# Reordering the dense steps of the second block: projections, transposes, scores, mixed values, feed-forward

## The chip, the cores and the metric

One core of a Trainium2 chip. The metric is the device time of one execution in microseconds (us). Five engines work side by side, each through its own queue in order: TensorE (PE) multiplies matrices, VectorE (DVE), ScalarE (ACT) and GpSimd (POOL) work element by element, SyncE (SP) issues DMAs. They wait for each other through semaphores.

## The reference

Two blocks work on x (2 batches of 1024 tokens, 256 features). The first block (attention over all tokens, then a mixture of 64 experts) isn't touched here. The second is `x = x + L1_ffn(L1_cond(x))`; L1_cond is a rotation of x, and L1_ffn has two layers of this form (cut):

```python
def _layer(x, wqkv, qs, ksc, wo, lg, lb, w1, b1, w2, b2):
    h = shift_token(x)                     # half of the features one token late
    q, k, v = split(h @ wqkv)              # 8 heads of 64
    q, k = l2norm(q) * qs, l2norm(k) * ksc
    q, k = rotary_xpos(q, k)               # cos/sin tables, times a scale by position
    o = local_attention(q, k, v)           # each token: itself and the 128 before
    x = x + o @ wo
    h = layernorm(shift_token(x)) * lg + lb
    a, g = split(h @ w1 + b1)
    return x + (a * gelu(g)) @ w2 + b2
```

Everything is float32.

## The kernel before

The second block runs over 32 windows of 128 tokens (2 layers x 2 batches x 8) and over 8 chunks of 512 tokens for the feed-forward. One loop, `for s in range(-2, WINDOWS)`, is a software pipeline: step s projects window s + 2, turns (transposes) queries and keys of window s + 1, scores window s, turns the softmax weights e of window s - 1, mixes values for window s - 2 or s - 1, and does a quarter of the feed-forward of a chunk that lags seven steps (LAG = 7). The order of the Python calls is the order on PE, DVE, ACT and POOL: `tc.manual_schedule` names these engines, so nothing is moved by a scheduler. Steps up to s = 4 also carry the rest of the first block (`beside`); from s = 5 to 29 a step is called dense; the last two are `late`.

The pieces, with the names that the profile uses (lines of the kernel before):

- `project(i)` L1146: pq, 4 matmuls of 128x128 by 512 (float32 goes twice through the array, so 8 records). `rotate_parts(i)`: ACT copies pq to raw (L1176) and squares it (sq, L1177), DVE multiplies pq by the cosines (L1164), POOL raw by the sines (t2, two operations, L1184). `norms(i)`: DVE sums the squares (L1193 and two small ones), POOL takes three Newton steps of four small operations (L1200 to L1203) to zn, the reciprocal norms. `rotated(i)`: DVE adds cosines and sines (L1209) and multiplies the keys by zn (L1210).
- `values(i)` L1216: pv, 2 matmuls; `keep_values(i)`: ACT copies it (L1226).
- `turn(i)`: 16 transposes of 64 rows into pt (L1231), two ACT copies to qT and kT (L1242); every third window POOL copies kT (L1247).
- `scores(i, hg)` L1259: sc for half the heads, matmuls of 64x64 by 192. `maxima(i, hg)`: DVE adds the mask, scales and takes the maximum (L1280, four each). `weights(i, hg)`: ACT takes exp (L1297, four each). `divide(i, hg)`: a DVE reciprocal (L1309), then four products (L1313), on POOL for hg 0 and on DVE for hg 1.
- `turn_e(i, hg)`: 16 transposes into pe (8 where the window is the first of its batch; L1231), copied to eT by ACT for hg 0 (L1334) and by DVE for hg 1 (L1332).
- `mix(i, hg)` L1347: po, 8 matmuls on 64 columns each; after hg 1 ACT copies to oT (L1358).
- `project_out(g)` L1367: pwo, 8 matmuls of 512, once in four windows, added on DVE (L1371); `halves(f)`: POOL adds the two feature halves (L1383).
- `forward(at)`: quarter k of chunk f. k = 0: gates 0, 1; k = 1: gates 2, 3; k = 2: gate 4, `centre` of the next chunk, gate 5; k = 3: `normalise`, `normalised` of the next chunk, `feed`. A `gate` is pga (L1436; the last, narrow one L1444), gelu on ACT (L1448), a product u on DVE (L1449). `centre` is pm (L1390), two subtractions on DVE (L1398), a square on ACT (L1400), a sum on POOL (L1402). `normalise` is pvar (L1390) and two ACT operations (L1410, L1411); `normalised` a product on DVE (L1417) and two operations on POOL (L1419). `feed` is py (L1463, L1468).
- `weights2(l, ...)`: DMAs of a layer's weights and tables on SP (L1044, L1052). For "tabs" it also issues four products on POOL (L1046) that scale the two tables by q_scale and k_scale. For the second layer it is called with "tabs" and "wqkv" in step 13, behind `norms` and ahead of `project_out` and `halves`.

PSUM banks in this block: `two_banks` hands out three pairs in turn, to pq, sc, pe, pt, pwo, pga and py in the order in which they are asked for, so each waits for the readers of the third one before it. `bank` hands out two single banks in turn, to pv, po, pm and pvar. eT has three buffers.

The order of PE's work in a dense step before: pq, sc (both halves), [mix of s - 2, what is left], pe of hg 0, pv, pt, [pwo], pe of hg 1, the quarter of the feed-forward.

Of the kernel before, what the change touches and what calls it, by code (L numbers as in the profile page):

```python
# [93 lines left out]
def tile_kernel(ctx: ExitStack, tc: tile.TileContext, a: dict, out: bass.AP):  # L94
# [899 lines left out]
    with tc.manual_schedule(  # L994
        engines={mybir.EngineType.PE, mybir.EngineType.DVE, mybir.EngineType.Activation}
    ):
        at_weigh = (1, 3, 4, 6)
        for g in range(2):
            weights(g)
        for it in range(3, ITS):  # L1000
            n, m = divmod(it, 8)
            if it + 1 < ITS:
                logits(it + 1)
            dispatch(it)
            if n and m in (1, 4):
                experts(4 * n - 4 + m // 4 * 2)

            i = it - ITS + 8
            if 0 <= i < 4:
                for jj in range(4):  # L1010
                    fetch(i, jj)
            if i - 1 in at_weigh:
                scale(at_weigh.index(i - 1))
            if i in at_weigh:
                heaviest(at_weigh.index(i))
                weigh(at_weigh.index(i))
        turn_w(0, 0)
        experts(12)
        turn_w(0, 1)
        combine(0, 0)  # L1020
        turn_w(0, 2)
        combine(0, 1)
        turn_w(0, 3)
        combine(0, 2)
        experts(14)
        dxs.close()
        for t in (xa, xb):
            nc.gpsimd.memset(t[:, :, :, 0:1], 0.0)


        load = {}
        wqo = pphi.tile([P, 4 * D * 4], F32, tag="phi", name="wqo")
        load["wqkv"] = wqo[:, : 6 * INNER].rearrange("p (k n) -> p k n", k=2)
        load["wo"] = wqo[:, 6 * INNER :].rearrange("p (k n) -> p k n", k=4)
        mask = dx0.tile([P, 2 * KEYS], F32, tag="l1", name="mask")
        nc.sync.dma_start(mask, a["mask"])

        def weights2(l, *names):
            for name in names:
                if name == "tabs":  # L1040

                    load[name] = [dx0.tile([P, 2, 8, DH], F32, tag="dsp", name=f"tabs{l}{y}") for y in range(2)]
                    for y, t in enumerate(load[name]):
                        nc.sync.dma_start(t, a["tabs"].rearrange("p (x y) w d -> y p x w d", y=2)[y])  # L1044
                        for x, of in enumerate((("qs", "ks"), ("qsr", "ksr"))[y]):
                            nc.gpsimd.tensor_tensor(  # L1046
                                t[:, x], t[:, x], bcast(rows[:, ROWS[f"{of}{l}"]], 1, 8), ALU.mult
                            )
                    continue
                k = {"wqkv": 2, "wo": 4, "w1": 2, "w2": NF}[name]  # L1050
                whole = HID // P if name == "w2" else k
                nc.sync.dma_start(  # L1052
                    load[name][:, :whole, :], a[name][l, : whole * P].rearrange("(c p) n -> p c n", p=P)
                )
                if whole < k:
                    for r0 in (0, TG):
                        nc.sync.dma_start(load[name][r0 : r0 + TAIL, whole, :], a[name][l, whole * P :])

        weights2(0, "wqkv", "tabs", "wo")
    with tc.manual_schedule(  # L1060
        engines={mybir.EngineType.PE, mybir.EngineType.DVE, mybir.EngineType.Activation}
    ):
# [35 lines left out]
    with tc.manual_schedule(  # L1098
# [125 lines left out]
        def keep_values(i):  # L1224
            vs[i] = la.tile([P, INNER], F32, tag="v", name="v", bufs=6)
            nc.scalar.copy(vs[i], pvs.pop(i))  # L1226
# [154 lines left out]
        def halves(f):  # L1381
            l, b, t0 = chunk(f)
            nc.gpsimd.tensor_tensor(  # L1383
                fa["sq"][:, 0, :], shifted(xb, 0, b, t0, 512), shifted(xb, 1, b, t0, 512), ALU.add
            )
# [138 lines left out]
                nc.vector.scalar_tensor_tensor(yo, py, col(f"b2{l}", c), yo, ALU.add, ALU.add)  # L1524
                nc.sync.dma_start(out[c * P : (c + 1) * P, b * S + t0 + lo : b * S + t0 + lo + m], yo)

        def forward(at):

            f, k = divmod(at, 4)
            if at == -1:  # L1530
                normalise(0)
            if not 0 <= f < CHUNKS:
                return
            if k == 0:
                gate(f, 0)
                gate(f, 1)
            if k == 1:
                gate(f, 2)
                gate(f, 3)
            if k == 2:  # L1540
                gate(f, 4)
                if f + 1 < CHUNKS:
                    centre(f + 1)
                gate(f, 5)
            if k == 3:
                if f + 1 < CHUNKS:
                    normalise(f + 1)
                    normalised(f + 1)
                feed(f)


# [28 lines left out]

        LAG = 7
        fa = {}
        for s in range(-2, WINDOWS):
            now, before, nxt, new = (0 <= s + d < WINDOWS for d in (0, -1, 1, 2))

            if new:
                project(s + 2)
                rotate_parts(s + 2)

            if s == LAG - 1:  # L1590
                centre(0)
            if s == LAG:
                normalised(0)
            ended = 0 <= s - 2 < WINDOWS

            late = s >= WINDOWS - 2
            dense = s > max(PARTS) and not late
            if ended and not dense and not late:  # L1600
                mix(s - 2, 1)
            if now and dense:
                for hg in range(2):
                    scores(s, hg)
            if ended and dense:
                for hg in range(2):
                    if (s - 2, hg) in eTs:
                        mix(s - 2, hg)
            if s == 5:
                rotate(3)  # L1610
            if now and not dense and not late:
                scores(s, 0)
                maxima(s, 0)
            beside(s, "a")
            if before:
                turn_e(s - 1, 0)
            if now and not late:
                if dense:
                    maxima(s, 0)
                weights(s, 0)  # L1620
            if new:
                values(s + 2)
                keep_values(s + 2)
            beside(s, "c")
            if ended and late:
                for hg in range(2):
                    if (s - 2, hg) in eTs:
                        mix(s - 2, hg)
            if now:
                for hg in () if dense else (0, 1) if late else (1,):  # L1630
                    scores(s, hg)
                for hg in (0, 1) if late else (1,):
                    maxima(s, hg)
                    if hg == 0:
                        weights(s, 0)
            if before and not dense:
                mix(s - 1, 0)
            if nxt:
                turn(s + 1)
            if now:  # L1640
                weights(s, 1)
            if new:
                norms(s + 2)
            if s + 2 == B * NWIN - 1:
                weights2(1, "tabs", "wqkv")
            beside(s, "b")
            if 0 <= s - 2 < WINDOWS and (s - 2) % 4 == 3:
                project_out((s - 2) // 4)
                if (s - 2) // 4 in halved:
                    halves((s - 2) // 4)  # L1650
            if before:
                turn_e(s - 1, 1)
            if now:
                divide(s, 0)
            if new:
                rotated(s + 2)
            if s == 5:

                f = xp.tile([P, 4 * NS], F32, tag="e", name="f")
                at = 0  # L1660
                for name, k, n in (("u", NF, 512), ("w2", NF, D), ("yo", 2, 512), ("rs", 1, 512), ("sq", 2, 512), ("gl", 2, 512)):
                    fa[name] = f[:, at : at + k * n].rearrange("p (k n) -> p k n", k=k)
                    at += k * n
                fa["rs"] = fa["rs"][:, 0, :]
                fa["hc"] = xin.tile([P, 2, 2, 512], F32, tag="x1", name="hc")
                load["w2"] = fa["w2"]
                load["w1"] = xp.tile([P, NE // 4 * D], F32, tag="y1", name="w1")[:, : 2 * W1N].rearrange(
                    "p (k n) -> p k n", k=2
                )
                weights2(0, "w1", "w2")  # L1670
            forward(s - LAG)
            if now:
                divide(s, 1)
            beside(s, "e")
            if s == B * NWIN + 2:
                weights2(1, "wo")
            if s == LAG + 4 * (CHUNKS // 2) - 2:
                weights2(1, "w1")
            if s == LAG + 4 * (CHUNKS // 2) - 1:
                weights2(1, "w2")  # L1680


        w, f = WINDOWS - 1, CHUNKS - 2
# [136 lines left out]
```

## Time and profile before

| | us |
|---|---|
| median of 3 runs | 1564.66 (1563.07 to 1564.69) |
| the profiled execution, device time | 1566.07 |
| its span, first to last instruction | 1563.9 |
| TensorE's mean granted clock | 0.997 |
| dense step 7 (gates 0 and 1), from pq to the next pq | 17.55 |
| dense step 21 (pwo, gate 4, centre, gate 5) | 23.90 |
| dense step 22 (normalise, feed) | 21.28 |

A line of the timeline gives start, modelled duration, engine, line of the kernel, operation, output <- inputs, the tile form (rows x columns), shape and count, and in brackets the idle time before it with what ended it. Ends on PE are modelled and overlap the next group; the distance from start to start is the time that a group takes. A line of the waits gives who waited for whom, the total in us, how many times, and the longest. The granted clock is the share of full speed that the chip let TensorE have.

### The profile page before, as it was taken

To read this page: it belongs to the slowest core of one execution; us is meant where nothing else is said; L and a number is where in the kernel's file an instruction comes from. 1 tells how busy PE (TensorE), PEld (TensorE's weight loads), DVE (VectorE), ACT (ScalarE), POOL (GpSimd) and SP (SyncE) were. 2 spreads that over 40 slices of the span, in tenths; PEclk is the share of its full clock that TensorE was granted. 3 is DMA by queue.
4 is the path that set the end of the run, shared out by engine and by line. 5 is a ranking of instruction groups with operands and counts; after the bars stand their busy time and mean duration, and the time that the engine had idled before them with its cause. 6 is when DMAs were issued, how large, how long until landed. Compare 5 with 4: busy or idle time off the path is not lost.

```text
span 1563.9 us, 25919 instructions
## 1 busy us (share of the span) xinstructions
PE 1543.9 (99%) x10176; PEld 753.1 (48%) x10176; DVE 885.4 (57%) x1606; ACT 881.3 (56%) x1710; POOL 526.7 (34%) x863
## 2 busy tenths in 40 slices
PE   8999999999999999999999999999999999999999
PEld 4333433333333444444776566555545454545544
DVE  5868768776873222225455756656556565656532
ACT  2478768787886222225233544766646666666641
POOL 4333323333330100000102344555555555555401
PEclk9999999999999999999999999999999999999999
DMA  5100010000000544445742102000100001000001
GB/s 163 55 14 14 1 21 8 6 16 8 2 1 28 167 139 152 148 151 181 241 128 88 55 1 84 2 1 1 68 1 1 15 1 51 6 1 28 14 15 40
DMA packets 49865, 82.80 MB, mean 53 GB/s; under 512 B 4552, under 2 KB 25328, under 8 KB 49488
## 3 DMA queue, kind: packets, MB, share of 16 engines
q1 hardware_dynamic: 47200, 75.31, 15.7%
q0 software_dynamic: 1584, 5.29, 1.1%
q8 instruction: 80, 1.31, 0.3%
q10 hardware_dynamic: 960, 0.56, 0.1%
q14 instruction: 41, 0.34, 0.1%
HBM read 55.97 MB, written 20.97 MB: 49 GB/s over the span
## 4 chain that ended last, share of the span: by engine, by line
PE 96%; DVE 1%; POOL 1%; ACT 1%; DMA 1%; issue 0%; ACTq 0%; DVEq 0%; POOLq 0%
PE sc L346 9%; PE pga L1436 9%; PE po L364 8%; PE pm L312 7%; PE lg L815 7%; PE pq L1146 7%; PE cmb L934 7%; PE sl L841 7%; PE py L1463 4%; PE pv L1216 4%; PE po L1347 4%; PE pwo L1367 3%; PE sc L1259 3%; PE pe L1231 2%; PE pqk L282 2%; PE py L862 2%
## 5 line engine op out<-in xcount | busy, mean ns | idle before, releaser
L319 DVE TENSOR_REDUCE mx<-pm 128x2 f32<-128x1024 f32 x256 | 301.5, 1219 | 108.1 <-PE pm L312 108.0
L354 ACT ACTIVATE e<-sc 128x512 f32<-128x512 f32 (+1 forms) x500 | 263.6, 614 | 67.8 <-PE pm L312 63.6
L346 PE MATMUL sc<-qs,km 32*128 32x512 f32 x1024 | 247.7, 616 | 0.7 <-ACT cg L564 0.7
L312 PE MATMUL pm<-km,qm 32*128 32x512 f32 x1024 | 242.8, 616 | 0.0
L382 POOL TENSOR_TENSOR ob<-ob,part 128x512 f32<-128x512 f32 x101 | 128.5, 1272 | 251.2 <-ACT part L381 251.2
L1436 PE MATMUL pga<-hc,w 128*128 128x512 f32 x320 | 143.8, 600 | 0.0
L364 PE MATMUL po<-e,v 128*32 128x512 f32 x1024 | 136.8, 604 | 0.0
L346 PEld LDWEIGHTS sc<-qs,km 32*128 32x128 f32 x1024 | 91.5, 183 | 86.6 <-ACT e L354 65.2
L1313 POOL TENSOR_SCALAR eall<-eall,den 128x192 f32<-128x192 f32 (+1 forms) x128 | 114.3, 906 | 26.9 <-DVE den L1309 26.9
L934 PE MATMUL cmb<-xb,y 128*128 128x256 f32 x512 | 118.7, 384 | 0.6 <-ACT xb L920 0.6
L1146 PE MATMUL pq<-wqo,xa 128*128 128x512 f32 x256 | 116.8, 599 | 2.2 <-ACT xb L920 1.2
L815 PE MATMUL lg<-phi,xa 128*128 128x512 f32 x256 | 116.1, 595 | 0.0
L841 PE MATMUL sl<-dsp,xb 128*128 128x512 f32 x256 | 114.9, 592 | 0.0
L1297 ACT ACTIVATE eall<-eall,nmx 128x192 f32<-128x192 f32 (+1 forms) x256 | 111.7, 442 | 4.3 <-DVE nmx L1280 4.1
L312 PEld LDWEIGHTS pm<-km,qm 32*128 32x128 f32 x1024 | 83.2, 183 | 49.3 <-DVE mx L319 35.0
L1184 POOL TENSOR_TENSOR t<-raw,tabs 128x512 f32<-128x512 f32 x64 | 80.6, 1281 | 75.1 <-ACT raw L1176 74.9
L825 DVE TENSOR_TENSOR l<-lg,keep 128x512 f32<-128x512 f32 x32 | 22.1, 692 | 144.8 <-ACT keep L823 144.8
L934 PEld LDWEIGHTS cmb<-xb,y 128*128 128x128 f32 x512 | 94.9, 189 | 17.7 <-issue 3.2
L1176 ACT COPY raw<-pq 128x1024 f32<-128x1024 f32 x32 | 32.4, 1013 | 110.5 <-PE pq L1146 109.8
L1436 PEld LDWEIGHTS pga<-hc,w 128*128 128x128 f32 x320 | 58.9, 190 | 68.1 <-issue 63.8
L1280 DVE CUSTOM_DVE_ANT_0 eall<-sc,mask,zn 128x192 f32<-128x192 f32 (+1 forms) x256 | 87.1, 404 | 4.8 <-PE sc L1259 4.7
L823 ACT COPY keep<-lg 128x512 f32<-128x512 f32 x32 | 18.7, 584 | 126.0 <-issue 105.4
(229 smaller groups left out, 2368.7 us busy)
## 6 DMA issues: line engine op xcount, KB each, us to landing
lgd<-keep SPq DMA_DIRECT2D x64, 256.0 KB, 2.4
w<-in_ffn_W SPq DMA_DIRECT2D x16, 1024.0 KB, 7.2
ebig<-lgd SPq DMA_DIRECT2D x64, 256.0 KB, 3.3
wqo<-in_wqkv SPq DMA_DIRECT2D x2, 1536.0 KB, 8.1
w<-in_w SPq DMA_DIRECT2D x2, 1386.0 KB, 7.5
km<-hk SPq DMA_DIRECT2D x32, 64.0 KB, 2.3
qm<-hq SPq DMA_DIRECT2D x32, 64.0 KB, 2.3
phi<-in_phi SPq DMA_DIRECT2D x1, 2048.0 KB, 7.4
```

Source lines behind the costliest of these rows:

```text
L312: nc.tensor.matmul(pm[:, x, :], qm[u % 2][r, i * P : (i + 1) * P], km[u % 3][r, n * 512 : (n + 1) * 512], start=True, stop=True,)
L319: nc.vector.tensor_reduce(mxs[hu][:, i % 4, 2 * half : 2 * half + 2, n], pm, AX.X, ALU.max)
L346: nc.tensor.matmul(sc[:, x, :] if both else sc[x], km[u % 3][r, j * P : (j + 1) * P], qs[u % 2][r, n * 512 : (n + 1) * 512], start=True, s ...
L354: nc.scalar.activation(part, t, AF.Exp, scale=1.0 / HD0**0.5)
L364: nc.tensor.matmul(po[32 * hh : 32 * hh + 32, :], v[b][:, j, at : at + 32], es[s, hh // 2][:, hh % 2, :], start=True, stop=True,)
L382: nc.gpsimd.tensor_tensor(obs[u, n], obs[u, n], part, ALU.add)
L815: nc.tensor.matmul(lg[:, b, :], xa[:, k, b, 1 + m * P : 1 + (m + 1) * P], phi[:, k, n * 512 : (n + 1) * 512], start=(k == 0), stop=(k == 1),)
L841: nc.tensor.matmul(accs[n][b][:, c, :], xo_tm[:, b * 8 + m, c * P : (c + 1) * P], d[:, b, :], start=(m == 0), stop=(m == 7),)
L934: nc.tensor.matmul(acs[q][:, c, :], y[b][:, 4 * jj + j, c * P : (c + 1) * P], eT[:, j // 2, j % 2 * 256 : (j % 2 + 1) * 256], start=(jj == ...
L1146: nc.tensor.matmul(pq[:, x, :], shifted(xa, k, b, w * WIN, P), load["wqkv"][:, k, x * 512 : (x + 1) * 512], start=(k == 0), stop=(k == 1),)
L1313: engine.tensor_scalar(e[:, x, c, lo:KEYS], e[:, x, c, lo:KEYS], den[:, x, c : c + 1], None, ALU.mult)
L1436: nc.tensor.matmul(pt[:, x, :], load["w1"][:, k, lo : lo + P], hcs[f][:, k, :], start=(k == 0), stop=(k == 1))
```

## The change

A function `dense_step(s)` takes over steps 5 to 29; the other steps keep the old order, without their dense branches. Its order on PE: pq, [what is left to mix of s - 2], [pwo], pv, pe of hg 0, pe of hg 1, pt, sc of both halves, po of window s - 1, the quarter of the feed-forward. `centre(0)` and `normalised(0)` of steps 6 and 7 stay at the head of the step. `forward` gets an argument `between`, called inside the quarter, through which `rotated(s + 2)` is issued. The scaling of the tables becomes a name of its own, "scales", issued behind `divide`, while the DMAs of tables and wqkv are issued behind `keep_values`. The tiles and DMAs of the feed-forward's weights are issued within step 5 rather than at its end.

```diff
+                    continue
+                if name == "scales":
+                    for y, t in enumerate(load["tabs"]):
                         for x, of in enumerate((("qs", "ks"), ("qsr", "ksr"))[y]):
                             nc.gpsimd.tensor_tensor(
                                 t[:, x], t[:, x], bcast(rows[:, ROWS[f"{of}{l}"]], 1, 8), ALU.mult
...
-        weights2(0, "wqkv", "tabs", "wo")
+        weights2(0, "wqkv", "tabs", "scales", "wo")
...
-        def forward(at):
+        def forward(at, between=lambda: None):
...
             if not 0 <= f < CHUNKS:
+                between()
                 return
             if k == 0:
                 gate(f, 0)
+                between()
                 gate(f, 1)
             if k == 1:
                 gate(f, 2)
+                between()
                 gate(f, 3)
             if k == 2:
+                between()
                 gate(f, 4)
...
                     normalised(f + 1)
+                between()
                 feed(f)
...
+        def dense_step(s):
             if s == LAG - 1:
                 centre(0)
             if s == LAG:
                 normalised(0)
+            project(s + 2)
+            rotate_parts(s + 2)
+            for hg in range(2):
+                if (s - 2, hg) in eTs:
+                    mix(s - 2, hg)
+            if s == 5:
+                rotate(3)
+            if (s - 2) % 4 == 3:
+                project_out((s - 2) // 4)
+                if (s - 2) // 4 in halved:
+                    halves((s - 2) // 4)
+            if s == 5:
+                feed_forward_tiles()
+            values(s + 2)
+            turn_e(s - 1, 0)
+            turn_e(s - 1, 1)
+            turn(s + 1)
+            keep_values(s + 2)
+            last = s + 2 == B * NWIN - 1
+            if last:
+                weights2(1, "tabs", "wqkv")
+            for hg in range(2):
+                scores(s, hg)
+            for hg in range(2):
+                maxima(s, hg)
+                weights(s, hg)
+            for hg in range(2):
+                mix(s - 1, hg)
+            norms(s + 2)
+            for hg in range(2):
+                divide(s, hg)
+            if last:
+                weights2(1, "scales")
+            forward(s - LAG, lambda: rotated(s + 2))
...
         for s in range(-2, WINDOWS):
...
+            if dense:
+                dense_step(s)
+                continue
...
-            if now and dense:
-                for hg in range(2):
-                    scores(s, hg)
-            if ended and dense:
-                for hg in range(2):
-                    if (s - 2, hg) in eTs:
-                        mix(s - 2, hg)
...
-            if s + 2 == B * NWIN - 1:
-                weights2(1, "tabs", "wqkv")
```

## The prediction

> **What bounds the kernel now.** First the page's busy times and its chain: TensorE (PE) is busy 99% of the span and holds 96% of the chain. No other engine is near it (DVE 57%, ACT 56%, POOL 34%), so only PE's own time counts: what its groups take, what it waits, and its clock.
>
> ```profile
> PE 1543.9 (99%) x10176; PEld 753.1 (48%) x10176; DVE 885.4 (57%) x1606; ACT 881.3 (56%) x1710; POOL 526.7 (34%) x863
> PE 96%; DVE 1%; POOL 1%; ACT 1%; DMA 1%; issue 0%; ACTq 0%; DVEq 0%; POOLq 0%
> ```
>
> Then PE's timeline of one ordinary step (s = 7). Start to start each group tells its true length, because the modelled ends overlap the next group.
>
> ```profile
> 1002.57 3.60 PE L1146 MATMUL pq<-wqo,xa 128*128 128x512 f32 x8
> 1006.10 1.53 PE L1259 MATMUL sc<-kT,qT 64*64 64x192 f32 x32
> 1007.56 1.97 PE L1347 MATMUL po<-eT,v 128*64 128x128 f32 x32
> 1009.46 0.71 PE L1231 MATMUL pe<-ident,eall 64*128 64x64 f32 x16
> 1010.10 1.98 PE L1216 MATMUL pv<-wqo,xa 128*128 128x512 f32 x4
> 1012.01 0.71 PE L1231 MATMUL pt<-ident,t 64*128 64x64 f32 x16
> 1012.56 0.66 PE L1231 MATMUL pe<-ident,eall 64*128 64x64 f32 x16
> 1013.15 7.13 PE L1436 MATMUL pga<-hc,w 128*128 128x512 f32 x16
> 1020.12 3.60 PE L1146 MATMUL pq<-wqo,xa 128*128 128x512 f32 x8
> ```
>
> No idle, 17.55 us. Inside a long row one full pass takes 0.427 us (pga pieces of the stage at 1220 to 1226 us: 0.85 for 2, 1.72 for 4). pv's 4 passes take 1.91 instead of 1.71: some 0.20 is the change of form, about 0.10 on the way in and 0.10 out. Transposes are 0.50 per 16, plus 0.05 in and 0.09 out (0.55 after pv and before pe, 0.64 between full forms).
>
> Third, PE's waits. The one large wait is at step 13, where the second layer's tables come in.
>
> ```profile
> PE pm L1390 <- POOL f L1383: 3.3, 1, 3.3
> ```
> ```profile
> 1133.64 6.38 POOL L1046 TENSOR_TENSOR tabs<-tabs,rows 128x512 f32<-128x512 f32 x4
> 1134.09 3.70 PE L1436 MATMUL pga<-hc,w 128*128 128x512 f32 x8
> 1139.99 1.09 POOL L1383 TENSOR_TENSOR f<-xb 128x512 f32<-128x512 f32 x1
> 1141.13 2.08 PE L1390 MATMUL pm<-f,ones_d 128*128 128x512 f32 x2 [3.34 <-POOL f L1383]
> 1143.00 3.62 PE L1444 MATMUL pga<-hc,w 128*106 128x512 f32 x4
> 1146.41 3.94 PE L1146 MATMUL pq<-wqo,xa 128*128 128x512 f32 x8
> ```
>
> Four scalings on POOL stand ahead of halves, which pm needs. After the wait L1444 takes 3.41 us for its usual 1.72: the granted clock is 0.50 for 6.8 us. The stretch from pga to the next pq is 12.32 us against 6.11 in the same stage at 1220.11, and pq itself 3.87 against 3.53: this seam costs 6.21 + 0.34 = 6.55 us.
>
> Last, how little idleness costs the clock.
>
> ```profile
> 892.41 0.71 PE L910 MATMUL pe<-ident,ebig 64*128 64x64 f32 x16 [0.87 <-DVE t L1164]
> 893.85 0.46 PE L1231 MATMUL pe<-ident,eall 64*128 64x64 f32 x8 [0.72 <-DVE nmx L1280]
> 894.24 3.55 PE L1216 MATMUL pv<-wqo,xa 128*128 128x512 f32 x4
> ```
>
> Waits of 0.87 and 0.72 us close together: the clock is 0.50 from 894.5 to 897.9, and pv takes 3.48 instead of 1.91. A wait of 0.61 beside 1.2 us of transposes (926.8 to 928.6) costs no clock. [...]
>
> **The change, part by part.** Times in a step are counted from the start of its first scores.
>
> Tables behind halves: the scalings move behind halves and behind the division of group 0, so the 6.55 us go. Late next are the scaled tables: on POOL the divisions end at 12.3, two scalings (1.3 to 1.6 each, L1046) at 15.2, the cosines (DVE 1.22) at 16.5. Step 14's turning of the queries and keys takes pq's bank and waits for them; it would stand at 15.8. Cost 0.6, bounds 0 and 2.5 (with a fall of the clock). Behind the scalings POOL has centre's addition (needed by pvar at 20.2, ready at 20.0), the copy of u's tail and the next sines; slower scalings would cost there, within the upper bound. On SP the DMAs of tables and wqkv have nothing behind them until wo, and start after the step's sines and after pv; wqkv has 11.3 us until the next pq (8.1 to land in the page), so it stays hidden. **-5.9** (-6.5 to -4).
>
> Rows: no instruction is added to PE, only groups change neighbours. An ordinary step becomes pq 3.42, pv 1.81 (no way in), pe 0.55, pe 0.50, pt 0.55, sc 1.46, po 1.90, pga 6.95 = 17.14, 0.41 less. But sc takes over the bank of the first pe, whose copy on ACT (1.01, L1334) starts 0.75 after that pe's start (L920 on the same form: 946.93 to 947.68) and ends at 1.76, 0.06 to PE: sc starts at 1.82 where it could at 1.60. All of PE's step is queued behind that wait. The second sc waits for DVE's copy (0.55 + 0.70 + 1.22 + 0.06 = 2.53) and could start at 2.55: nothing. 0.19 is left, x16 steps = 3.0. In a step with pwo two rows are joined: 23.90 becomes 23.13, less 0.22: 0.55 x3; x3 of 0.77 where only one window is turned, and the copy is 0.59. With steps 5, 6 and 7 (0.53, 0.19, 0.19) the rows bring **-7.9**. The passage from pt to sc is in no row; I take that of transposes into po (0.59 at 1482.00) and as bounds none and the 0.12 of the way into a full form: -10 to -4, if sc's wait doesn't hide it.
>
> New waits at the seams: turning e of group 0 needs POOL's division, and the old order had 20.9 us between sc and it; now it has the gates, pq and pv between, 15.5 us. Chain (durations from the groups of DVE, ACT and POOL between 960 and 1470 us): maxima 0.9 to 3.6 (8 of 0.338), sum of squares and two small ones 1.7, Newton on POOL 3.5 (12 small operations, 978.09 to 981.59), zn at 8.8, divisions to 12 or 12.7. That is enough where gates stand between, not in three places. Step 6 (only pm and pq, pv stand between: 10.4): DVE's rotated waits for zn (9.55), centre's two subtractions behind it end at 10.85, ACT's square 1.06, and queued behind that square raw 1.01, sq 1.06, the copy of e 1.01: sc at 15.07 instead of 12.2: +2.85. Step 7: rotated, normalised 1.22, cosines, then raw, sq, the copy: sc at 15.25 instead of 12.25: +3.0. Step 30, where project and values are over (pe at 9.5): rotated, u of gate 4 (0.75), the subtractions, the square, gelu 0.69, u of gate 5: the second sc at 14.5 and po at 15.3 instead of 11.5; 0.3 idle there falls away: +3.5. Each empties PE for some 3 us within 4.5, so by the row at 893 the clock falls once for 3.4 us, 1.7 lost each. That of step 6 lies in step 7's wait and costs nothing more: +3.4 (0 to 8). Together **+12.7** (8 to 18).
>
> [...]
>
> [...]
>
> w1, w2 and the other tiles of the feed-forward are issued earlier in step 5, used in step 7; the last mix of a window moves from the step after next to the next; every one of their instructions was there before. Nothing.
>
> Sum: -5.9 - 7.9 + 12.7 = -1.1 us. The profiled execution took 1566.07 (span 1563.9 and 2.2 around it) and would take 1565.0; it lies 1.4 above the median shown, 1564.66, so the median becomes 1563.6.
>
> **The rivals.** (a) The seams cost no clock, and about half their wait (POOL divides at 0.75 instead of 0.94, subtractions come earlier): -1.1 - 3.4 - 4 = 1556. For it: the 0.61 waits cost nothing. Against: three chains of in-order queues, worked out from rows. [...] (c) The rows save nothing, as the passages cost the same wherever they stand: +7.9, 1571.5. Against: pga to pq (6.97 for 6.83) pays on one side only.
>
> **How the numbers follow.** Forecast 0.45, (a) 0.23, (b) 0.15, (c) 0.17. Likeliest: 1563.6, on its own 1558 to 1570. Within 0.2% (3.1 us, about what a measurement here can tell from no change) lie 0.30, nearly all the forecast's; faster 0.32: (a) and 0.09 of the forecast; slower 0.38: (b), (c) and 0.06. The range takes in (a) and (c) and leaves out most of (b): 1556 to 1578.
>
> **What would show it.** Tables right: PE's wait pm <- POOL gone, no clock of 0.50 in step 13. Rows right: pq, pv, pe, pe, pt, sc, po in 10.4 us from pq's start to pga's, with 0.2 of wait before sc <- ACT eT. Seams right: PE waits of about 3 us in steps 6, 7 and 30, first on POOL's division, then on ACT's copy, with the clock at 0.50 behind. Wrong: no such waits (then (a)), or a granted clock under 0.98 between 1050 and 1450 us (then (b)).

## The result, and the profile after

| | us |
|---|---|
| median before (4 runs beside it) | 1564.68 (1563.07 to 1566.69) |
| median after (4 runs) | 1576.41 (1576.06 to 1577.68) |
| ratio, 95% interval | 1.0082 (1.0070 to 1.0095) |
| span of the profiled execution, before and after | 1563.9 and 1574.2 |

The change made the kernel 0.8% slower. Three single executions far from all others (2229.5 us with e2, 3966.0 with e9, 2753.6 of the kernel before beside e15) are left out of every ratio here and below. The page of the changed kernel, its busy times and its chain by engine:

```profile
PE 1541.1 (98%) x10176; PEld 756.0 (48%) x10176; DVE 883.3 (56%) x1606; ACT 881.7 (56%) x1710; POOL 535.9 (34%) x863
PE 90%; DVE 4%; POOL 2%; ACT 2%; issue 1%; DMA 1%; ACTq 0%; POOLq 0%; DVEq 0%
```

The number of instructions on each engine is the same and PE is 2.8 us less busy, but its part of the chain fell from 96% to 90%: DVE, POOL and ACT now stand in it. PE's waits between 800 us and the end say where (who waited for whom: total, times, longest):

```profile
PE pe L1234 <- POOL eall L1316: 7.3, 11, 1.7
PE pt L1234 <- DVE t L1167: 4.5, 5, 1.3
PE pe L1234 <- DVE f L1452: 2.2, 3, 0.7
...
PE sc L1262 <- ACT eT L1337: 0.6, 1, 0.6
```

The wait of pm on POOL (3.3) is gone. The division of the exponentials (L1316) is the largest new one, the cosines (L1167) and u (L1452) are the others, and once the copy of the turned exponentials (L1337): 14.6 us of waits in place of 3.3. (All lines are later by three: L1231 of before is L1234.)

PE's timeline in steps 6 and 7 of the changed kernel:

```profile
990.68 3.60 PE L1149 MATMUL pq<-wqo,xa 128*128 128x512 f32 x8
994.11 1.88 PE L1219 MATMUL pv<-wqo,xa 128*128 128x512 f32 x4
996.84 0.28 PE L1234 MATMUL pe<-ident,eall 64*128 64x64 f32 x2 [0.85 <-POOL eall L1316]
997.58 0.27 PE L1234 MATMUL pe<-ident,eall 64*128 64x64 f32 x2 [0.47 <-POOL eall L1316]
...
1000.74 1.11 PE L1234 MATMUL pt<-ident,t 64*128 64x64 f32 x16
1001.78 2.83 PE L1262 MATMUL sc<-kT,qT 64*64 64x192 f32 x32
...
1015.22 0.27 PE L1234 MATMUL pe<-ident,eall 64*128 64x64 f32 x2 [1.09 <-POOL eall L1316]
...
1018.82 2.84 PE L1262 MATMUL sc<-kT,qT 64*64 64x192 f32 x32 [0.60 <-ACT eT L1337]
```

The first transposes come two by two, each pair behind one product of POOL (0.74 us apart): 2.16 us idle in step 6 and 2.03 in step 7, where sc waits another 0.60 for ACT's copy. Behind each of the two seams sc takes 2.8 us instead of 1.46. The windows of these two steps (length, PE's busy time and records, PEld, DVE, ACT, POOL, and then PE's granted clock) give the clock's price:

```profile
988.86:1008.47 19.61, 17.43 (x135) 10.36 (x134) 13.38 (x41) 12.14 (x34) 10.27 (x21) 0.83 0.00 1
1008.47:1030.67 22.20, 19.51 (x142) 10.76 (x141) 13.77 (x36) 13.93 (x29) 16.84 (x34) 0.92 0.01 1
```

The time lost is the part of the clock that was not granted: 0.17 x 19.61 + 0.08 x 22.20 = 5.1 us, more than the waits (4.8).

An ordinary step (s = 12):

```profile
1110.29 3.60 PE L1149 MATMUL pq<-wqo,xa 128*128 128x512 f32 x8
1113.72 1.88 PE L1219 MATMUL pv<-wqo,xa 128*128 128x512 f32 x4
1115.54 1.21 PE L1234 MATMUL pe<-ident,eall 64*128 64x64 f32 x32
1116.58 0.66 PE L1234 MATMUL pt<-ident,t 64*128 64x64 f32 x16
1117.36 1.59 PE L1262 MATMUL sc<-kT,qT 64*64 64x192 f32 x32
1118.88 1.97 PE L1350 MATMUL po<-eT,v 128*64 128x128 f32 x32
1120.78 7.13 PE L1439 MATMUL pga<-hc,w 128*128 128x512 f32 x16
1127.75 3.60 PE L1149 MATMUL pq<-wqo,xa 128*128 128x512 f32 x8
```

17.46 us, 0.09 less than before (17.55). pt to sc is 0.78 where 0.55 would do: the wait for ACT's copy of pe.

The step behind a centring (s = 10; pvar and feed) has stalls that the old order had not. First the three groups of transposes before, without a wait, then PE of the changed kernel, then its DVE in the stretch that leads to the stalls:

```profile
1066.70 0.71 PE L1231 MATMUL pe<-ident,eall 64*128 64x64 f32 x16
...
1069.26 0.71 PE L1231 MATMUL pt<-ident,t 64*128 64x64 f32 x16
1069.81 0.66 PE L1231 MATMUL pe<-ident,eall 64*128 64x64 f32 x16
```

```profile
1075.00 0.71 PE L1234 MATMUL pe<-ident,eall 64*128 64x64 f32 x16
1076.43 0.71 PE L1234 MATMUL pe<-ident,eall 64*128 64x64 f32 x16 [0.72 <-DVE f L1452]
1077.95 0.71 PE L1234 MATMUL pt<-ident,t 64*128 64x64 f32 x16 [0.81 <-DVE t L1167]
1078.68 1.53 PE L1262 MATMUL sc<-kT,qT 64*64 64x192 f32 x32
```
```profile
1068.98 1.21 DVE L1212 TENSOR_TENSOR t<-t,t 128x1024 f32<-128x1024 f32 x1
1071.19 0.69 DVE L1213 TENSOR_TENSOR t<-t,zn 128x512 f32<-128x512 f32 x1 [1.00 <-POOL zn L1206]
1071.80 0.75 DVE L1452 SCALAR_TENSOR_TENSOR f<-pga,cols,f 128x512 f32<-128x512 f32 x1
1072.46 1.28 DVE L1401 TENSOR_TENSOR hc<-xb,pm 128x512 f32<-128x512 f32 x2
1075.63 0.74 DVE L1452 SCALAR_TENSOR_TENSOR f<-pga,cols,f 42x512 f32<-42x512 f32 x1 [1.89 <-ACT f L1451]
1076.67 1.23 DVE L1167 TENSOR_TENSOR t<-pq,tabs 128x1024 f32<-128x1024 f32 x1 [0.29 <-ACT raw L1179]
```

Read downwards it is one chain: the rotation waits for zn; u of gate 4 and the centring's subtractions stand behind it on DVE, ACT's square behind these (it starts at 1073.83), gelu 5, raw, and only then u of gate 5 and the cosines. PE's second pe takes the banks of gate 5, pt those of pq; both wait.

The reckoning, from the start of pq in one step to the start of pq in the next (steps 5 to 29; the last stretch ends at pvar of step 30). e1, e2 and so on are the experiments below.

| steps | before | after | e1 | e2 | e3 | e14 | e15 |
|---|---|---|---|---|---|---|---|
| 5 to 7 | 52.42 | 63.92 | 52.43 | 52.42 | 64.00 | 52.42 | 52.43 |
| 8 to 10 | 60.98 | 62.06 | 60.97 | 64.18 | 60.60 | 60.97 | 62.62 |
| 11 to 14 | 86.94 | 81.00 | 81.53 | 80.99 | 81.04 | 81.21 | 79.65 |
| 15 to 18 | 78.62 | 79.64 | 78.62 | 79.64 | 78.17 | 78.62 | 78.09 |
| 19 to 22 | 80.39 | 80.59 | 80.39 | 80.60 | 79.65 | 80.39 | 79.65 |
| 23 to 26 | 78.63 | 79.64 | 78.62 | 79.63 | 78.16 | 78.62 | 78.09 |
| 27, 28 | 35.20 | 35.01 | 35.21 | 35.01 | 35.01 | 35.21 | 35.01 |
| 29 to pvar | 30.52 | 33.14 | 30.51 | 33.16 | 34.06 | 30.51 | 29.56 |
| sum | 503.70 | 515.00 | 498.28 | 505.63 | 510.69 | 497.95 | 495.10 |

One thing to know for it: the new order mixes values one window earlier, so the stretch in which it begins holds one more po (1.90 us) and the last one less. After minus before is +11.3: +9.6 in steps 5 to 7, -2.8 in 8 to 28, +4.5 at the end (each without that 1.90). The rest of the kernel has the same order, but step 5 starts anywhere from 964.97 us (e14) to 967.90 (e7), in part because the clock falls around 894 us in some profiles and not in others (from 894.5 to 897.9 us it is 0.50 in the profile of before and 1.00 in that of the changed kernel); so traces are compared by this table and the medians by their intervals.

### The profile page after: what moved, and what is told of

Read it like the earlier page. It is cut to its first block, busy times and chain, and to the rows that moved or that the text cites. A ratio compares the mean times of both kernels' runs of the same rounds, so it can differ in the third digit from the quotient of the medians.

```text
span 1574.2 us, 25888 instructions
## 1 busy us (share of the span) xinstructions
PE 1541.1 (98%) x10176; PEld 756.0 (48%) x10176; DVE 883.3 (56%) x1606; ACT 881.7 (56%) x1710; POOL 535.9 (34%) x863
## 4 chain that ended last, share of the span: by engine, by line
PE 90%; DVE 4%; POOL 2%; ACT 2%; issue 1%; DMA 1%; ACTq 0%; POOLq 0%; DVEq 0%
PE sc L346 9%; PE po L364 8%; PE pga L1439 8%; PE pm L312 7%; PE lg L815 7%; PE cmb L934 7%; PE sl L841 7%; PE pq L1149 6%; PE py L1466 4%; PE pwo L1370 3%; PE po L1350 3%; PE sc L1262 3%; PE pv L1219 3%; PE pqk L282 2%; PE py L862 2%; PE pe L1234 1%
## 5 line engine op out<-in xcount | busy, mean ns | idle before, releaser
L1316 POOL TENSOR_SCALAR eall<-eall,den 128x192 f32<-128x192 f32 (+1 forms) x128 | 121.3, 961 | 16.3 <-DVE den L1312 16.3
```

What stands on the lines that cost most here:

```text
L1316: engine.tensor_scalar(e[:, x, c, lo:KEYS], e[:, x, c, lo:KEYS], den[:, x, c : c + 1], None, ALU.mult)
```

## The experiments

Theory at the start: the time is lost where DVE's, ACT's and POOL's queues run late for transposes that the new order asks for earlier (steps 6 and 7, the steps behind a centring, step 30), and the scalings' new place gains. Rivals: the new order costs by itself wherever it stands, or PE's own passages and clock do.

| | median us | ratio to before, 95% interval |
|---|---|---|
| e1 tables alone | 1560.18 | 0.9975 (0.9965 to 0.9985) |
| e2 old order in 5 to 7 | 1568.21 | 1.0023 (1.0013 to 1.0033) |
| e3 centre first | 1570.58 | 1.0035 (1.0023 to 1.0048) |
| e4 mended 5 to 7 | 1569.62 | 1.0029 (1.0017 to 1.0041) |
| e5 old order in 29 | 1574.17 | 1.0068 (1.0047 to 1.0089) |
| e6 e2, e3 and e5 together | 1559.50 | 0.9982 (0.9970 to 0.9994) |
| e7 scores first | 1589.10 | 1.0162 (1.0133 to 1.0191) |
| e8 e7, cosines' scaling on DVE | 1590.31 | 1.0168 (1.0140 to 1.0196) |
| e9 mended | 1559.30 | 0.9973 (0.9964 to 0.9982) |
| e10 e1, cosines' scaling on DVE | 1559.10 | 0.9971 (0.9962 to 0.9980) |
| e11 e9 again | 1559.24 | 0.9968 (0.9955 to 0.9981) |
| e12 tables ahead | 1577.09 | 1.0079 (1.0056 to 1.0102) |
| e13 gates first | 1558.08 | 0.9972 (0.9961 to 0.9983) |
| e14 e10 again | 1558.64 | 0.9974 (0.9964 to 0.9983) |
| e15 square late | 1556.44 | 0.9952 (0.9938 to 0.9966) |

Before itself had medians from 1562.28 to 1564.77 beside them. The medians of e1, e2, e4, e6, e12 and e15 lie 0.2 to 1.2 us above the range of the theory that they are taken to support; there the waits and the table decide. Where a theory failed, the text says so.

**e1, the tables alone.** On the kernel before, with the scalings a name of their own as in the change:

```diff
                 divide(s, 0)
+            if s + 2 == B * NWIN - 1:
+                weights2(1, "scales")
```

> The order of before in every step, and only the scalings of the second layer's tables moved behind halves and behind the division of group 0 in step 13. Theory (the tables gain by themselves what step 13 shows in the changed kernel, 6.65 us, less up to 0.9 for scaled tables that come late in step 14): 1558 to 1559 us, the 3.34 us wait of pm on POOL gone and no granted clock of 0.50 near 1137. Rival (the scalings only move the wait, to the cosines of step 14 or to the sum for pvar): 1563 to 1565, with a new wait of 2 to 3 us in step 14.

1560.18. Step 13 takes 23.90 instead of 30.11, and step 14 22.42 instead of 21.63, since the cosines' table is late for it:

```profile
1136.78 1.02 PE L1393 MATMUL pm<-f,ones_d 128*128 128x512 f32 x2
...
1147.37 0.71 PE L1234 MATMUL pe<-ident,eall 64*128 64x64 f32 x16 [1.06 <-DVE t L1167]
```

pm waits for nothing now, pe of step 14 waits 1.06 us. Net -5.4 in the table. The move pays on the old order, though the median is 1.2 us above the expected range.

**e2, the old order in steps 5 to 7.**

```diff
-                dense_step(s)
+                (dense_step if s > LAG else old_step)(s)
```

> The changed kernel, but with the order of before in steps 5, 6 and 7; the new order begins in step 8. Theory (the seam of steps 6 and 7 costs 4.8 us of waits and 5.1 us of fallen clock, because no gates stand there between a window's scores and the turning of its exponentials): 9 to 10 us below the changed kernel, 1566 to 1568. Rival (the loss belongs to the new order itself and shows in whichever steps are the first with it): the waits on POOL's division move to step 8, and the time stays at 1573 or above.

1568.21. The waits of steps 6 and 7 went and did not come back in step 8 (its whole increase in the table is the 1.90 of the extra po, and 0.2): -9.4 in the table. The loss belongs to the place, not to being first.

**e3, centre first.**

```diff
             if k == 2:
+                if f + 1 < CHUNKS:
+                    centre(f + 1)
                 between()
                 gate(f, 4)
-                if f + 1 < CHUNKS:
-                    centre(f + 1)
                 gate(f, 5)
```

> The changed kernel, but in the steps with gates 4 and 5 the centring of the next chunk is issued ahead of both gates and ahead of the rotation that waits for POOL's Newton steps; every instruction stays. Theory (in these steps DVE stands still for zn with the subtractions queued behind it, so ACT's square, gelu 5, u of gate 5, raw and the cosines all come late for the transposes of the next step): the PE waits pe <- DVE f L1452 (2.2 us in 3) and pt <- DVE t (4.5 us in 5) nearly go, 5 to 6.7 us off, 1570 to 1571.5. Rival (ACT's row of exponentials, table loads and gelu sets the end whatever DVE does): waits of the same size behind ACT, 1575 to 1577.

1570.58. The wait on u is gone, that on the cosines 2.2 in 4 instead of 4.5 in 5 (1.4 of it the late table of step 14); steps 10, 18 and 26 are 1.5 us shorter each, step 22 0.9; the last stretch is 0.9 longer. Not one instruction was added or taken away: the place of the centring in the queues, on DVE above all, made these stalls.

**e4, the new order in steps 5 to 7 with shorter chains.**

```diff
-            engine = nc.vector if hg else nc.gpsimd
+            engine = nc.vector if hg or i in (5, 6) else nc.gpsimd
...
-            ahead = i == LAG + 2
+            ahead = False
...
+            if at == -2:
+                centre(0)
```

(`centre(0)` leaves the head of step 6, and `normalised(0)` goes behind `rotate_parts` in step 7.)

> The changed kernel with the new order kept in steps 5 to 7, but their chains shortened: DVE divides both groups of windows 5 and 6 (POOL divides none), the first centring is issued ahead of step 5's rotation, in step 7 raw goes ahead of the cosines and the normalising product behind them. Theory (the waits of steps 6 and 7 are DVE, ACT and POOL in their own order, not PE's order of groups): the waits on POOL's division go, at most 1.6 us of wait is left in each of the two steps, the clock falls once or not at all, 1566 to 1569. Rival (transposes in a row leave PE too idle by themselves, or another chain takes over): 1573 or above, still with a clock of 0.50 in both steps.

1569.62. Waits of 0.42 us are left in step 6, 1.04 in step 7, and the clock is 1.00 in both (14.60 and 18.71 us from pm's or pq's start to the next pq, against 19.61 and 22.20). The same PE order, with earlier data, keeps its clock: it was the queues, and these rows of transposes (1.6 us, with 0.42 and 0.30 us of wait beside them) kept the clock at 1.00.

**e5, the old order in step 29** (the condition of e2 as `s < 29`).

> The changed kernel, but with the order of before in step 29. Theory (in step 30 no projections stand between the gates and the turning of window 29's exponentials, so it waits 3.1 us on POOL's division and the clock falls once, 1.7 us): 4 to 5 us below the changed kernel, 1571.5 to 1572.5, the last wait on POOL's division (1.71 us) and those after it gone. Rival (whatever step is the last with the new order hands its lateness to the next): the same waits one step earlier or later, 1575 or above.

1574.17, less than expected. The last stretch is 3.4 us shorter (29.72), not 4.8: where the order changes, one po is missing between sc and pe, and pe waits 1.05 us for the cosines. And step 10 is 1.65 us longer than in the changed kernel, with the same instructions and the same waits:

```profile
1075.90 0.71 PE L1234 MATMUL pe<-ident,eall 64*128 64x64 f32 x16 [0.72 <-DVE f L1452]
1077.42 0.71 PE L1234 MATMUL pt<-ident,t 64*128 64x64 f32 x16 [0.81 <-DVE t L1167]
1078.15 2.70 PE L1262 MATMUL sc<-kT,qT 64*64 64x192 f32 x32
```

In the changed kernel sc behind these two waits took 1.53; here 2.70, with a granted clock of 0.72 from 1077 to 1080 us. So a stall of this size cost a fall of the clock in one execution and not in the other. e12 has the fall too (2.58).

**e6, the three together.**

> The changed kernel with the order of before in steps 5 to 7 and in step 29, and the centring ahead of gates 4 and 5: the three edits of e2, e3 and e5 together. Theory (the three losses are separate places): their sum, 8.2 and 5.8 as measured and about 4.5, off 1576.4: 1557 to 1559, a little under e1 (1560.2), because the rows then bring what is left of them, 0.09 in each ordinary step and 0.43 in each with pwo. Rival (the rows bring nothing, as passages cost the same wherever they stand): 1560 to 1562.

1559.50. The sum of the stretches is 498.3, as e1, though three waits were left or new: the scaled cosines in step 14 (1.37), pm behind pwo in step 29 (1.84; centre first and the old order don't go together) and pq's bank (1.05). The losses are separate places and add up. Whether rows gain was not decided.

**e7 and e8, scores first.**

```diff
             project(s + 2)
             rotate_parts(s + 2)
...
+            values(s + 2)
+            for hg in range(2):
+                scores(s, hg)
...
                     mix(s - 2, hg)
...
                 project_out((s - 2) // 4)
...
-            values(s + 2)
             turn_e(s - 1, 0)
             turn_e(s - 1, 1)
             turn(s + 1)
...
-            for hg in range(2):
-                scores(s, hg)
...
-            for hg in range(2):
-                mix(s - 1, hg)
```

(The work of DVE, ACT and POOL is spread over the step much as in the order of before, and `rotated` stands ahead of the quarter again.) e8 is e7 with the cosines' two scalings on DVE.

> The changed kernel with another order in its dense steps: projections in a row, then scores, then the mixed values of the window before last (as in before), then wo's products, and only then the transposes in a row and the feed-forward. Groups of like form stay together as in the change, but no group reads what was turned in the same step, and the exponentials are turned a whole step after their scores. Theory (the rows save 0.41 in an ordinary step as summed, and the change lost it to waits that its dependences make): ordinary steps 17.1 to 17.25, no wait on POOL's division, none in steps 6, 7 and 30, 1551 to 1554. Rival (a change of form costs the same wherever it stands, so rows save nothing): ordinary steps 17.45 to 17.55 without any wait, 1558 to 1561.

> e7, with the two scalings of the second layer's cosines given to DVE in step 13, POOL keeping those of the sines. Theory (in step 14 the cosines wait for POOL's four scalings, 1.06 us in e1): 0.5 to 1.1 us below e7, no wait on DVE's cosines in step 14. Rival (DVE waits for the tables' transfer and holds back what is behind it): as e7 or up to 2 us above it, with a wait of PE late in step 13.

1589.10 and 1590.31: both theories were far off. The seams went, as argued, but the new places made new waits, which two lines of e7's PE in steps 12 and 13 show:

```profile
1117.36 7.13 PE L1439 MATMUL pga<-hc,w 128*128 128x512 f32 x16 [0.97 <-ACT eT L1337]
...
1134.70 7.13 PE L1370 MATMUL pwo<-oT,wqo 128*128 128x512 f32 x16 [1.70 <-ACT oT L1361]
```

wo's products stand right behind the po that they need, and the copy of po stands on ACT behind four exponentials (it starts at 1134.09 us); the gates take the bank of pe, whose copy stands behind that. What e7 does tell is the price of the rows themselves: step 12, 18.25 us, is 17.28 without its wait, so the rows save some 0.27 in an ordinary step, not the 0.41 that was summed. e8 was 1.2 above e7, inside both intervals; it shows nothing on the tables.

**e9 and e10, and e11: rows mended against no rows.** e9 has the old order in steps 5 to 7, centre first, and

```diff
-            engine = nc.vector if hg else nc.gpsimd
+            engine = nc.vector if hg or i == 29 else nc.gpsimd
...
-                            nc.gpsimd.tensor_tensor(
+                            (nc.gpsimd if y or not l else nc.vector).tensor_tensor(
```

e10 is e1 with the second of these edits; e11 is e9 once more, and its profile is the one that is read.

> The changed kernel with all that the runs so far point to: the order of before in steps 5 to 7, the new order from step 8 to 29 with the centring ahead of gates 4 and 5, both groups of window 29 divided by DVE, and the scalings of the second layer's cosines given to DVE. Theory (what e6 still waits goes: 1.37 us for the scaled cosines in step 14, 1.84 for the sum behind pwo and 1.05 for pq's bank in step 29): 3 to 4 us below e6 (1559.5), 1555 to 1557, below both kernels and below e10. Rival (these waits come back as others, or DVE's two scalings hold back u and the rotation): 1558.5 to 1560.

> e1 with the scalings of the second layer's cosines given to DVE: the order of before everywhere, so that e9 less e10 is what the new order of groups brings by itself once its waits are mended. Theory (the 1.06 us wait of step 14 for the scaled cosines goes, and rows bring 0.09 in each ordinary step, 0.43 in each with pwo): 0.8 to 1.1 us below e1 (1560.2), 1559 to 1559.5, and e9 some 3 us below it. Rival (rows bring nothing): e9 and e10 within 1 us.

> The kernel of e9 once more, for a profile of it: in e9 the time was 1559.3 against e10's 1559.1, where 3 us less were expected. Theory 1 (the rows bring nothing: ordinary steps of 17.46 to 17.55 without the waits named in e9): 1558 to 1560, PE's waits on the cosines and on pm gone. Theory 2 (the waits came back as others): 1558 to 1560, with 2 to 4 us of PE waits between 1020 and 1490 us. If 1555.5 to 1557: the runs of e9 were high.

1559.30, 1559.10 and 1559.24: no difference, and e10 is only 0.33 us better than e1 in the table (step 14 22.08 instead of 22.42). The profile of e11 decides for the second theory, waits that came back as others: steps 8 to 28 are 3.3 us shorter than e10's (the extra po taken off), but step 30 has

```profile
1455.19 0.71 PE L1234 MATMUL pe<-ident,eall 64*128 64x64 f32 x16
1458.43 2.84 PE L1262 MATMUL sc<-kT,qT 64*64 64x192 f32 x32 [2.53 <-DVE f L1452]
```

With the divisions on DVE and the centring first, ACT's square (1.06 us, at 1454.53) and a table load (1.28) stand ahead of gelu 4, and u of gate 5 comes at 1458.

**e12, the tables ahead.** The changed kernel, with the scalings back in front of `halves`:

```diff
+            if s + 2 == B * NWIN - 1:
+                weights2(1, "tabs", "scales")
             if (s - 2) % 4 == 3:
                 project_out((s - 2) // 4)
```

> The changed kernel with the four scalings of the second layer's tables put back ahead of halves, where before had them; all else as changed. Theory 1 (the order of groups alone takes pm's wait away: wo's products and the sum of halves now come some 10 us ahead of pm, so the scalings, 5 to 6.4 us from the landing of the tables at about 1140, end before pm at 1148.6): 1575 to 1576.5, no wait of pm on POOL, and 1.3 us less wait for the cosines in step 14. Theory 2 (as in the prediction, it is the scalings' place that gains 5.9 us): 1581 to 1583, the wait of 3.3 us before pm back and the clock fallen behind it.

1577.09, beside 1576.41 for the changed kernel: the first theory. Step 13 takes 23.46 us in both. POOL in step 13 of e12, and PE:

```profile
1140.62 4.98 POOL L1049 TENSOR_TENSOR tabs<-tabs,rows 128x512 f32<-128x512 f32 x4 [4.25 <-DMA tabs<-in_tabs]
1145.54 1.11 POOL L1386 TENSOR_TENSOR f<-xb 128x512 f32<-128x512 f32 x1
```
```profile
1139.39 1.88 PE L1219 MATMUL pv<-wqo,xa 128*128 128x512 f32 x4
...
1149.97 1.02 PE L1393 MATMUL pm<-f,ones_d 128*128 128x512 f32 x2
```

The sum of halves waits behind the scalings as ever and ends at 1146.65; pm comes at 1149.97, because pwo ends 10.6 us ahead of it now (it stood right before pe and gate 4). In the changed kernel the scalings' move gained nothing, and step 14 is 0.37 us longer with it (22.52 against 22.15), since the cosines' table is later: either edit removes the wait, and the gain was put down to one of them.

**e13 and e14: gates first.** e13 is e9 with this in place of centre first, e14 is e10 once more:

```diff
             if k == 2:
-                between()
                 gate(f, 4)
+                gate(f, 5)
                 if f + 1 < CHUNKS:
                     centre(f + 1)
-                gate(f, 5)
+                between()
```

> e9, but in the steps with gates 4 and 5 the order is gate 4, gate 5, centring, rotation, so that no u waits behind the subtractions, the square's table or zn. Theory (e11's profile: steps 8 to 28 are 3.3 us shorter than e10's once the po that changes its step is counted, and step 30 loses them again, 2.53 us of wait for u of gate 5 and 1.7 of clock): 1555 to 1556, the wait sc <- DVE f gone, clock 1.00, 3 to 4 us below e10 run beside it. Rival (the wait of step 30 comes back in another place, or rows bring nothing): 1558.5 to 1560, within 1 us of e10.

> e10 once more, beside e13 on the same chip, for the comparison: 1558.5 to 1559.5 by both theories.

1558.08 and 1558.64. The wait for u went; another took its place in step 30 (so the rival's first half came true):

```profile
1456.46 1.53 PE L1262 MATMUL sc<-kT,qT 64*64 64x192 f32 x32
1459.99 1.98 PE L1350 MATMUL po<-eT,v 128*64 128x128 f32 x16 [2.01 <-ACT eT L1337]
```

The copy of window 29's exponentials is issued behind the centring's square on ACT, and po behind the wait takes 1.91 us to the next group for its 16 records, where po at 1477.34 takes 1.03.

**e15, the square late.** e13, and

```diff
+            if f != 6:
+                square(f)
...
             if before:
                 turn_e(s - 1, 0)
+            if s == 30:
+                square(6)
```

> e13, but the square of the chunk centred in step 29 and POOL's addition behind it are issued in step 30, behind the copy of window 29's first exponentials, which ACT now makes ahead of it. Theory (e13's profile: step 30 waits 2.01 us for that copy, which stands behind the square on ACT, and the clock falls behind it; steps 6 to 29 are 1.9 us shorter than without rows): wait and fall go, 2.5 to 3 us below e13 (1558.1), 1555 to 1556, ratio to before 0.9950 to 0.9960, and 3 to 4 us below e14 (1558.6). Rival (the square is then late for pvar, or rows bring nothing on the clock's side): 1557.5 to 1559, with a wait of pvar on POOL.

1556.44, ratio 0.9952 (0.9938 to 0.9966): the fastest of all, and faster than both kernels. All of its waits of PE from step 8 on that the view lists are 0.6 (three) on the cosines, and 1.2 in step 30; the clock there is 1.00. It is 2.85 us below e14 in the table; by the ratios 0.22%, 3.4 us, with intervals that just overlap (0.9964 and 0.9966). Of the 2.85, 0.8 is e14's one wait, for the scaled cosines in step 14 (22.10 us against 21.18, where step 22 differs by 0.10 only). e15 also has other places for gate 5 and the square, but e14's PE has no other wait there that these could take away. So the rows themselves bring some 2 us, the end included.

## Why the prediction was wrong, point by point

"Rows" are the groups of like form put side by side, "seams" the steps 6, 7 and 30, where less work than usual stands between a window's scores and the turning of its exponentials.

| part | predicted | measured, from the table |
|---|---|---|
| tables behind halves | -5.9 | -6.15 |
| rows in steps 8 to 28 | -6.45 | +3.33 |
| steps 5 to 7, rows and seams | +6.64 | +9.60 |
| steps 29 and 30, rows and seams | +4.65 | +4.52 |
| sum | -1.1 | +11.30 |

(Tables: step 13 fell by 6.65, of which 0.44 is what step 21, of the same kind, saves as well, and step 14 grew by 0.06 more than step 22. Rows: -2.82 in steps 8 to 28 less the tables' -6.15. The predicted parts are the prediction's own terms, sorted by step: 16 x 0.19, 2 x 0.55 and 3 x 0.77 lie in steps 8 to 28, one 0.55 in step 29.)

**Tables: right in size, wrong in cause.** The wait (3.34 us) went, with the clock of 0.50 behind it (1.00 in step 13 of the changed kernel), and step 14 pays for late cosines (1.30 us of wait, against 0.81 in step 22). But the prediction gave the gain to the scalings' place; that the number fits is in part luck. e1 shows that this place is enough, e12 that the order of groups is enough without it. The working looked at POOL's queue for pm and not at when the changed order asks for halves.

**Rows: the step that failed.** "0.19 is left, x16 steps = 3.0" took every step without pwo for an ordinary one. With the tables' gain taken out, steps 8 to 28 became 3.33 us longer where 6.45 were to be saved. Three things came in its place.
- Steps 10, 14, 18, 22 and 26, behind a centring, wait for u of gate 5 and for the cosines (6.2 of the 6.7 us in two lines of the waits, DVE f and DVE t; 0.5 is step 14's late table). The prediction followed DVE's chain at the seams and for the tables' cosines, but not here, where the same chain ends 1.5 us late. e3 took most of the stalls away by the centring's place alone. In a round of eight steps (15 to 22) before takes 159.01, after 160.23, e15 157.74.
- An ordinary step saves 0.09. The wait of sc on ACT's copy was there as worked out (pt to sc 0.78, where 0.55 + 0.22 was summed); sc itself took 1.52 instead of 1.46, and the rest is 0.02 here and there.
- The passages cost more than 0.41 would have it: without waits e7 saves 0.27. So the rows are worth about half of what was summed, in e15 1.3 us in a round of eight steps where 2.5 were predicted. Rival (c), "the rows save nothing", had more in it than its 0.17.

**Seams: right in place, a clock too few.** The waits of 2.85 and 3.0 us in steps 6 and 7 were 2.16 and 2.63. What failed is "That of step 6 lies in step 7's wait and costs nothing more": a late sc makes everything behind it late, step 7's own chain with it, so the 3.3 us of step 6's clock were paid, and then 1.8 for step 7's, where 1.7 had been put in for both. Step 6's fall was also twice as long as the one at 893 us from which the 1.7 was taken: the clock is 0.50 from about 998.4 to 1005.0 us. e2 and e4 show that the waits are the cause. At step 30, 3.12 us of waits and 1.7 of clock came where 3.5 and 1.7 were predicted.

**Rivals.** (a) needed seams without a fall of the clock; it fell at all three (0.83 and 0.92 over steps 6 and 7, 0.50 from 1477 to 1479 us in step 30). (b), a clock that falls in the ordinary steps (under 0.98 between 1050 and 1450 us), was the author's supposition, and no run shows it: the granted clock there was 1.00. The feature that would show the seams, waits first on POOL's division and then on ACT's copy, was there in step 7 with 2.03 and 0.60.

**Not decided.** How the 0.14 us between 0.27 and 0.41 divides among the passages; and by how much exactly e15 is faster than e14, where the intervals overlap.

## What to carry to other kernels

When a group on the bounding engine is moved earlier, work out its data's chain in every kind of step, not only in the odd ones, since what had slack in one order is late in the other and a step's kind is set by the quarter before it. Follow an in-order queue downwards: one instruction that waits (a product that needs zn) delays all that is queued behind it, on engines that never see the cause (in step 10 DVE's 1.00 us for zn stand at the head of the chain for which PE waits 0.72 and 0.81). And where two edits would each remove the same wait, the gain is counted once.

## What the runs showed of the hardware

**The clock fell on small stalls, and not always on the same ones.** Idle of 0.72 and 0.81 us within 3 us left the clock at 1.00 in the changed kernel's step 10; in e5's it was 0.72 from 1077 to 1080 us and 0.71 from 1080 to 1083, in e12's 0.79 and 0.65 (sc 1.53, 2.70, 2.58). The row at 893 us on which the prediction built its price is such a case itself: the same two waits (0.87 and 0.73) in the changed kernel leave pv at 1.91 us, at a clock of 1.00, where before it took 3.48. Single waits of 1.70 (e7, six times) and 1.84 (e6, once) cost no time behind them (wo's products took 7.06 or 7.07 us behind the first, 7.06 in e1 without a wait; pm 0.96 behind the second, as in e11). Behind 2.01 (e13) and 2.53 (e11), once each, po took 1.91 for 1.03 and sc 2.77 for 1.46, in e11 at a mean clock of 0.81 from 1455 to 1464 us. What decides which stall costs the clock, no run shows.

**A small POOL operation took six times its time beside DVE's sum.** POOL's Newton steps in step 6 of the changed kernel, and DVE's addition that starts with the slow one:

```profile
991.41 0.33 POOL L1205 TENSOR_SCALAR nt<-nt 128x16 f32<-128x16 f32 x1
991.83 1.30 POOL L1206 TENSOR_TENSOR zn<-nt,z 128x16 f32<-128x16 f32 x1
993.21 0.21 POOL L1203 TENSOR_TENSOR nt<-zn 128x16 f32<-128x16 f32 x1
```
```profile
991.83 1.22 DVE L1212 TENSOR_TENSOR t<-t,t 128x1024 f32<-128x1024 f32 x1
```

0.2 to 0.3 us each, but 1.30 for the one that starts together with DVE's sum of two arrays (1.22); the same at 1008.85 (1.30) and at 1069.02 (1.24). In the chains that steps 6 and 7 wait for, and in the steps with gates 4 and 5, the new order has that sum beside the Newton steps, and so zn, and the division behind it, came 1.1 us later. The kernel before has such slow operations too (1.21 at 1002.14, beside DVE's sum at 1002.09), but no wait of PE on the division, and none in the Newton steps from which the prediction read 3.5 us (978.09 to 981.59). Between 940 and 1500 us all 13 of these sums that run beside Newton steps in the changed kernel, and all 12 before, have one such slow operation (1.07 to 1.30 and 1.12 to 1.21 us); every other operation of the Newton steps took 0.35 us or less.
